# Five rooms instead of three for the transposed probabilities of heads 2 to 13

## The chip, the cores and the metric

The kernel runs on one core of a Trainium2 chip. The metric is device time in microseconds (us) of one execution; the median of several runs is compared. TensorE (PE) multiplies and transposes, VectorE (DVE) and ScalarE (ACT) work on what it leaves in PSUM, GpSimd (POOL) does elementwise work in SBUF, and SyncE (SP) issues nearly all DMAs.

## The reference

One transformer block on a sequence of 2048 rows of 1024 numbers, in float32: layer norm, attention with 16 heads of 64 and rotary embedding over a causal mask, output projection, layer norm and residual; then a gated feed-forward part with 2752 inner columns whose weights come as 4-bit codes with a scale for each 64, again with norms and residual.

```python
x = x + _layernorm(_L0_attn_ref(_layernorm(x, axis=-1), Wq, Wk, Wv, Wo), axis=-1)
x = x + _layernorm(_L0_ffn_ref(_layernorm(x, axis=-1), gate_codes, gate_scales, up_codes, ...), axis=-1)
...
logits = jnp.where(causal, logits, MASK_VAL) / jnp.sqrt(jnp.float32(HEAD_DIM))
attn = jax.nn.softmax(logits, axis=-1)
out = jnp.einsum('bhqk,bhkd->bhqd', attn, v)
```

## The kernel before

Matmuls take their operands as a rounded part and a remainder (fp32r, "hi" and "lo"); `split` makes the two: a cast on ACT (L118) and a subtraction on DVE (L119). A full product is three matmuls (`mm3`, L112 to L114).

The heads are worked off in pairs. For a head and a block of 512 queries (J), `scores` multiplies q by k (L273, L275) into one of three PSUM banks tagged "S", takes negated row maxima on DVE (L279, L281), exponentials on ACT (L283, `prob`), sums and reciprocals on DVE, and scales the probabilities on POOL (L305). `weighted` then goes over blocks of 128 keys (kb): four transposes (L315) put the probabilities of the block into one of three PSUM banks tagged "T" (`pt`); `split` casts and subtracts them into an SBUF room `pw` of 4 KB a partition, hi and lo; two matmuls (L319 with hi, L320 with lo) add the block to the output bank `o`. At the end ACT copies the lower half of `o` (L322) into `ol`, of which there is one room, DVE adds (L323) and SP stores it (L324). There are 640 such blocks, 480 of them in heads 2 to 13.

Between these instructions stand projections for later heads: `qkv` (L112 to L114 on `xc`, blocks of x loaded at L218, and on weights `w` cast by L184 from loads at L177).

SBUF is shared out as rooms by tag. `SLOTS` gives the number of rooms and KB of each: "pw" has 3 rooms of 4 KB, "pb" 2 of 4 KB. A new tile of a tag takes the room of the tile as many tiles back as the tag has rooms, and its first writer waits until that one's readers are done. "pb" holds weights of the second pair early on (until before head 2), and rows of the output projection (`y`, written at L467) from heads 14 and 15 on; between them it lies unused. 

The order of the instructions on each engine is not that of the source. A scheduler places them when the kernel is built, by its own account of durations and of free rooms and banks (`schedule_with_timeline_sim=True`), with priorities by place in the source and a few anchors that pace projections (`pace`, `after`). Each engine then runs its list in order. On the chip semaphores hold an instruction until its inputs and rooms are ready, and everything behind it on that engine waits as well.

Of the kernel before, what the change touches and what calls it, by code (L numbers as in the profile page):

```python
# [11 lines left out]
FR = mybir.dt.float32r  # L12
# [12 lines left out]
P = 128  # L25
KE = E // P
# [31 lines left out]
def block_kernel(ctx, tc, x, wq, wk, wv, wo, gu_codes, gu_scales, d_codes, d_scales, cos_sin, out):  # L58
# [15 lines left out]
    def slot(tag, shape, dtype, name):  # L74
        assert int(np.prod(shape[1:])) * 4 <= SLOTS[tag][1] * 1024, (tag, shape)
        return sb.tile(shape, dtype, tag=tag, name=name, bufs=SLOTS[tag][0])

    def bank(tag, name="bk"):
        return ps.tile([P, 512], F32, tag=tag, name=name, bufs=BANKS[tag])
# [37 lines left out]
    def split(hi, lo, src):  # L117
        A.copy(hi, src)  # L118
        return V.tensor_tensor(lo, src, f32(hi), ALU.subtract)  # L119
# [137 lines left out]
    def scores(J, q, k, anchors):  # L257
# [47 lines left out]
                    G.tensor_scalar(p, p, rc[:, jj % BATCH, i : i + 1], 0.0, ALU.mult, ALU.add)  # L305
        return prob

    def weighted(h, J, prob, v):
        o = bank("O", "o")
        nk = 4 * J + 4  # L310
        for kb in range(nk):
            j0 = max(0, kb - 4 * J)
            pt = bank("T", "pt")
            for j in range(j0, 4):
                T.transpose(pt[:, j * P : (j + 1) * P], prob[kb // 4][:, j, kb % 4 * P : (kb % 4 + 1) * P], ident)  # L315
            cs = slice(j0 * P, 512)
            pw = slot("pw", [P, 2, 512], FR, "pw")
            split(pw[:, 0, cs], pw[:, 1, cs], pt[:, cs])
            T.matmul(o[:, cs], lhsT=v[:, kb, :], rhs=pw[:, 0, cs], start=kb == 0, stop=False)  # L319
            T.matmul(o[:, cs], lhsT=v[:, kb, :], rhs=pw[:, 1, cs], start=False, stop=kb == nk - 1)  # L320
        ol = slot("ol", [D, 512], F32, "ol")
        A.copy(ol, o[D:P, :])  # L322
        V.tensor_tensor(ol, o[:D, :], ol, ALU.add)  # L323
        load(at[J][h * D : (h + 1) * D, :], ol)  # L324
# [45 lines left out]
    def attend(h, J, q, k, v, anchors):  # L370
        weighted(h, J, scores(J, q, k, anchors), v)
# [12 lines left out]
    for pair in range(KE - 1):  # L384
# [3 lines left out]
        for h in (2 * pair, 2 * pair + 1):  # L388
# [10 lines left out]
            for i, J in enumerate(order):  # L399
# [4 lines left out]
                if i % 2 == 0:  # L404
                    two = order[i : i + 2]
# [428 lines left out]
```

## Time and profile before

| what | value |
|---|---|
| median of 3 runs | 3020.89 us (3020.09 to 3022.32) |
| the profiled execution | 3012.18 us |
| its span | 3010.4 us |
| mean granted PE clock | 0.992 |
| PE, DVE, ACT, POOL busy | 97%, 68%, 56%, 32% of the span |
| all casts L118 of `pw` | 640, 324.1 us on ACT |
| all subtractions L119 of `pw` | 640, 378.4 us on DVE |
| all transposes L315 | 2176, 345.4 us on PE |

Busy time of an engine counts what its instructions cover. In a line of groups or waits, `A <- B: t, n, m` says that A sat idle until B ended, t us in total, n times, m us at the longest. A line of stretches gives the stretch, its length, busy us of PE, PEld (weight load), DVE, ACT and POOL with the number of instructions, then the granted PE clock, the busy share of the DMA engines and GB/s. A line of the chain gives start, length and what. Heads 2 to 13 fall into about 330 to 1345 us of the span.

### The profile page before, as it was taken

To read this page: it belongs to the slowest core of one execution; us is meant where nothing else is said; L and a number is where in the kernel's file an instruction comes from. 1 tells how busy PE (TensorE), PEld (TensorE's weight loads), DVE (VectorE), ACT (ScalarE), POOL (GpSimd) and SP (SyncE) were. 2 spreads that over 40 slices of the span, in tenths; PEclk is the share of its full clock that TensorE was granted. 3 is DMA by queue.
4 is the path that set the end of the run, shared out by engine and by line. 5 is a ranking of instruction groups with operands and counts; after the bars stand their busy time and mean duration, and the time that the engine had idled before them with its cause. 6 is when DMAs were issued, how large, how long until landed. Compare 5 with 4: busy or idle time off the path is not lost.

```text
span 3010.4 us, 42538 instructions
## 1 busy us (share of the span) xinstructions
PE 2912.1 (97%) x14168; PEld 2406.1 (80%) x14168; DVE 2032.5 (68%) x4171; ACT 1697.9 (56%) x3569; POOL 954.8 (32%) x1055
## 2 busy tenths in 40 slices
PE   7989999999998999999999999999999999999998
PEld 6868888787877787777787888888888888888886
DVE  6567778787867677777666667776666677444347
ACT  4256667776766666676565555655555566333234
POOL 5344344443444343454332121222221223100034
PEclk9999999999999999999999999999999999999999
DMA  8787665657557558472356344434434444744446
GB/s 295 271 255 233 213 214 186 213 171 226 157 196 195 172 176 254 139 229 90 123 178 230 109 138 139 154 129 140 135 121 135 139 151 151 255 140 144 150 144 234
DMA packets 271740, 536.01 MB, mean 178 GB/s; under 512 B 22944, under 2 KB 113056, under 8 KB 255648
## 3 DMA queue, kind: packets, MB, share of 16 engines
q1 hardware_dynamic: 269344, 529.10, 54.3%
q10 hardware_dynamic: 2176, 4.19, 0.4%
q8 instruction: 112, 1.84, 0.3%
q14 instruction: 108, 0.88, 0.1%
HBM read 371.98 MB, written 161.22 MB: 177 GB/s over the span
## 4 chain that ended last, share of the span: by engine, by line
PE 79%; DMA 9%; DVE 5%; ACT 2%; issue 1%; POOL 1%; SPq 1%; POOLq 0%; ACTq 0%; DVEq 0%
PE bk L112 14%; PE bk L114 14%; PE bk L113 14%; PE pt L315 6%; PE qkv L112 4%; PE qkv L114 4%; PE qkv L113 4%; PE o L320 3%; PE o L319 3%; PE s L273 3%; PE s L275 3%; PE pj L466 2%; PE pj L464 2%; PE pj L465 2%; DMA wf<-in_wq 2%
## 5 line engine op out<-in xcount | busy, mean ns | idle before, releaser
L305 POOL TENSOR_SCALAR prob<-prob,rc 128x512 f32<-128x512 f32 (+3 forms) x640 | 404.9, 659 | 440.1 <-DVE rc L300 231.0
L112 PE MATMUL bk<-x,wt 128*128 128x512 f32 x1376 | 534.1, 390 | 4.6 <-ACT x L118 3.7
L113 PE MATMUL bk<-x,wt 128*128 128x512 f32 x1376 | 535.9, 389 | 0.0
L114 PE MATMUL bk<-x,wt 128*128 128x512 f32 x1376 | 535.7, 389 | 0.0
L283 ACT ACTIVATE prob<-s,mxs 128x512 f32<-128x512 f32 (+3 forms) x640 | 402.6, 633 | 145.9 <-DVE mxs L281 88.7
L119 DVE TENSOR_TENSOR pw<-pt,pw 128x512 fp32r<-128x512 f32 (+3 forms) x640 | 378.4, 601 | 119.7 <-ACT pw L118 117.9
L529 ACT ACTIVATE ln<-cs,bias 128x512 f32<-128x512 f32 x520 | 359.8, 716 | 107.0 <-DVE mb L535 20.4
L118 ACT CAST pw<-pt 128x512 fp32r<-128x512 f32 (+3 forms) x640 | 324.1, 527 | 169.6 <-PE pt L315 137.0
L315 PE MATMUL pt<-ident,prob 128*128 128x128 f32 x2176 | 345.4, 275 | 7.3 <-DVE pw L119 6.0
L315 PEld LDWEIGHTS pt<-ident,prob 128*128 128x128 f32 x2176 | 267.6, 141 | 62.0 <-issue 7.7
L112 PEld LDWEIGHTS bk<-x,wt 128*128 128x128 f32 x1376 | 258.4, 188 | 59.1 <-ACT x L118 3.9
L114 PEld LDWEIGHTS bk<-x,wt 128*128 128x128 f32 x1376 | 258.7, 188 | 53.9
L113 PEld LDWEIGHTS bk<-x,wt 128*128 128x128 f32 x1376 | 258.8, 188 | 53.5
L281 DVE TENSOR_REDUCE mxs<-s 128x1 f32<-128x512 f32 x384 | 260.9, 681 | 58.6 <-PE s L275 57.3
L273 PE MATMUL s<-k,q 128*128 128x512 f32 (+3 forms) x640 | 265.0, 415 | 23.9 <-ACT prob L283 19.7
L320 PE MATMUL o<-pw,v 128*128 128x512 f32 (+3 forms) x640 | 247.0, 388 | 8.3 <-DVE pw L119 7.6
L319 PE MATMUL o<-pw,v 128*128 128x512 f32 (+3 forms) x640 | 243.8, 381 | 8.6 <-ACT pw L118 6.7
L112 PE MATMUL qkv<-xc,w 128*128 128x512 f32 x576 | 230.9, 401 | 11.8 <-ACT w L184 6.3
L113 PE MATMUL bk<-bt,at 128*128 128x512 f32 x616 | 239.6, 389 | 0.0
L114 PE MATMUL bk<-bt,at 128*128 128x512 f32 x616 | 238.8, 389 | 0.0
L112 PE MATMUL bk<-bt,at 128*128 128x512 f32 x616 | 238.6, 389 | 0.0
L275 PE MATMUL s<-k,q 128*128 128x512 f32 (+3 forms) x640 | 235.6, 371 | 0.0
(150 smaller groups left out, 5504.7 us busy)
## 6 DMA issues: line engine op xcount, KB each, us to landing
xc<-xd SPq DMA_DIRECT2D x96, 1024.0 KB, 9.1
q<-qs SPq DMA_DIRECT2D x128, 256.0 KB, 6.8
ast<-S SPq DMA_DIRECT2D x44, 512.0 KB, 3.7
cs<-in_gu_scales SPq DMA_DIRECT2D x172, 128.0 KB, 3.2
cs<-in_gu_codes SPq DMA_DIRECT2D x86, 256.0 KB, 3.0
A<-in SPq DMA_DIRECT2D x66, 256.0 KB, 2.1
S<-in SPq DMA_DIRECT2D x66, 256.0 KB, 3.1
ast<-A SPq DMA_DIRECT2D x33, 512.0 KB, 4.5
```

What stands on the lines that cost most here:

```text
L112: r = T.matmul(o, lhsT=w[:, 0], rhs=xx[:, 0], start=first, stop=False)
L113: T.matmul(o, lhsT=w[:, 0], rhs=xx[:, 1], start=False, stop=False)
L114: T.matmul(o, lhsT=w[:, 1], rhs=xx[:, 0], start=False, stop=last)
L119: return V.tensor_tensor(lo, src, f32(hi), ALU.subtract)
L273: mm = T.matmul(s, lhsT=q[:, 0, j * P : (j + 1) * P], rhs=k[:, b:e], start=True, stop=False)
L275: T.matmul(s, lhsT=q[:, 1, j * P : (j + 1) * P], rhs=k[:, b:e], start=False, stop=True)
L283: A.activation(prob[i][:, j, : e - b], s, AF.Exp, bias=mx, scale=sign, accum_out=sums[:, j % BATCH, i : i + 1])
L305: G.tensor_scalar(p, p, rc[:, jj % BATCH, i : i + 1], 0.0, ALU.mult, ALU.add)
L315: T.transpose(pt[:, j * P : (j + 1) * P], prob[kb // 4][:, j, kb % 4 * P : (kb % 4 + 1) * P], ident)
L319: T.matmul(o[:, cs], lhsT=v[:, kb, :], rhs=pw[:, 0, cs], start=kb == 0, stop=False)
L320: T.matmul(o[:, cs], lhsT=v[:, kb, :], rhs=pw[:, 1, cs], start=False, stop=kb == nk - 1)
L529: A.activation(ln, c8, AF.Prelu, bias=bias_of[ab], scale=ab[0], alpha=ab[2])
```

## The change

`weighted` counts its blocks in `parts_made`. In heads 2 to 13 (`KE` is 8) two of every five blocks take their room from "pb" instead of "pw". With three rooms of "pw" and two of "pb", a block there takes the room of the block five back instead of three back. The numbers of rooms, the instructions and their sizes stay as they are.

```diff
+    parts_made = [0]
+
     def weighted(h, J, prob, v):
         o = bank("O", "o")
         nk = 4 * J + 4
@@
             cs = slice(j0 * P, 512)
-            pw = slot("pw", [P, 2, 512], FR, "pw")
+
+            parts_made[0] += 1
+            two = 2 <= h < 2 * KE - 2 and parts_made[0] % 5 > 2
+            pw = slot("pb" if two else "pw", [P, 2, 512], FR, "pw")
             split(pw[:, 0, cs], pw[:, 1, cs], pt[:, cs])
```

## The prediction

> **What bounds the kernel now.** I read the page first, then its engines by stretch, then the waits inside the stretch that the change touches (330 to 1345 us, heads 2 to 13), then the chain there.
>
> ```profile
> span 3010.4 us, 42538 instructions
> PE 2912.1 (97%) x14168; PEld 2406.1 (80%) x14168; DVE 2032.5 (68%) x4171; ACT 1697.9 (56%) x3569; POOL 954.8 (32%) x1055
> ```
>
> The stretch (its length, then busy us of PE, PEld, DVE, ACT, POOL, the granted clock, DMA share, GB/s):
>
> ```profile
> 330.00:1345.00 1015.00, 973.61 (x5301) 806.88 (x5300) 770.99 (x1995) 688.43 (x1824) 430.43 (x590) 0.99 0.63 195
> ```
>
> TensorE (PE) is the bound. In the stretch it idles 1015.0 - 973.6 = 41.4 us. Nothing in this change alters how much PE has to do, so only that idle time, and the clock lost after it, can be won.
>
> Who waits, in the stretch, for PE and then for ScalarE (ACT):
>
> ```profile
> PE s L273 <- ACT prob L283: 15.1, 23, 2.1
> PE qkv L112 <- ACT w L184: 5.4, 3, 3.9
> PE o L319 <- ACT pw L118: 5.1, 4, 2.6
> PE qkv L112 <- DMA xc<-xd: 4.8, 4, 1.8
> PE o L320 <- DVE pw L119: 4.6, 14, 0.7
> ```
>
> ```profile
> ACT pw L118 <- PE pt L315: 98.9, 134, 5.0
> ...
> ACT pw L118 <- PE o L320: 23.3, 15, 3.7
> ...
> ACT ol L322 <- DMA at<-ol: 11.5, 6, 2.4
> ```
>
> The wait for a free room is the line "ACT pw L118 <- PE o L320": the cast waits until the second weighted matmul of the block three back has read its room, 15 times, 23.3 us. No line of PE's is that wait; PE waits for the exponentials (L283), for weights (L184) and x blocks from DMA, and for casts and subtractions.
>
> What PE does in the three longest room waits (ACT resumes at 524.2, 662.5 and 820.0 us):
>
> ```profile
> 520.00:525.00 5.00, 5.00 (x31) 4.40 (x30) 0.71 (x6) 1.30 (x4) 4.13 (x7) 1.00 0.85 290
> 658.00:663.00 5.00, 5.00 (x26) 4.04 (x25) 1.45 (x3) 1.88 (x6) 0.00 (x0) 1.00 0.39 131
> 816.00:821.00 5.00, 5.00 (x26) 4.08 (x25) 1.31 (x3) 1.67 (x5) 0.00 (x0) 1.00 0.41 133
> ```
>
> PE (second number) is busy in all of the 5 us: it runs projection matmuls, and the hold on ACT costs nothing there. Last, the longest pieces of the chain that ended last in this stretch:
>
> ```profile
> 527.01 9.37 DMA at<-ol
> ...
> 729.71 13.64 DMA wf<-in_wq
> ...
> 931.23 12.17 DMA wf<-in_wq
> ...
> 1250.01 8.86 DMA at<-ol
> ```
>
> They are loads of weights, and the store of a head's output, whose single room `ol` holds up the next head's copy on ACT.
>
> **The change part by part.** *Removed: the room wait.* With five rooms I laid the built orders of both kernels side by side. In the old order 45 of the 480 casts of heads 2 to 13 have their transposes placed ahead of the matmul that frees their room; in the new one none has. So the wait does go away: between 0 (what the three stretches show) and 23.3 us (if every hold were on the path, and a little more with the clock). Following each PE wait of over 0.06 us back from releaser to releaser, I find one that passes through such a hold, at 430.9 us, 0.39 us. I take **-0.4 us**. The rooms are free: the weights in `pb` are last read long before head 2 (PE's 142nd us of work against the 328th), and the first row block that reuses `pb` is written at 1378.4 us, after head 13.
>
> *Moved: the order.* The scheduler places instructions by its own account of time, so freeing rooms reorders 4,308 of the 14,168 PE instructions, 126 of SP's and 74 of POOL's by a few places, up to the 1515th us of PE's work, past heads 14 and 15 too. PE's work is the same (2,832 us at 227 ns a 512-column matmul, 110 ns a transpose, by the starts in the trace). I count, for each weighted matmul, how much PE work lies between the end of its block's transposes and itself (its lead), and give each class of lead the mean stall that class had in the trace (time between starts above those figures):
>
> ```
> lead us            <0.5   0.5-1  1-1.5  1.5-2  2-2.5  2.5-3  3-4
> first (L319) old   3      10     36     74     77     36     103
>  stall us in all   2.3    0.6    3.8    3.9    1.6    0.9    2.2
>  new               1      5      34     66     83     51     95
> second (L320) old  3      0      11     18     65     72     92
>  stall us in all   1.5    0      2.5    0.1    5.4    2.1    1.5
>  new               1      2      7      18     49     75     103
> ```
>
> At the old means the first lose 2.1 us and the second 2.9: **-5.0 us**. The same for score matmuls against the one three back in their PSUM bank: 31 old leads under 2 us with 16.8 us of stalls become 33, 28 of 2 to 2.5 us become 37, 67 of 2.5 to 3 become 53: **+0.4 us**. These means hold only as far as the causes do: most of the score stalls are ACT held by something else. Bounds of this part: -30.2 (all stalls of weighted matmuls, longer leads included, gone) and +5 (the classes' means are no better than their mirror).
>
> *The store of a head's output.* ACT's copy L322 waits for the landing of the store before. In the trace that comes 11 to 12 us after the end of the earlier output's last matmul (679.0 to 690.1, 836.5 to 847.4, 524.2 to 536.4, 1248.1 to 1258.9), and the copy is late where two outputs end closer. In the new order short pairs come closer still: 5.99 to 5.19 us of PE work, 5.76 to 5.19 twice, 4.98 to 3.39, 6.81 to 5.56, and three new ones near 6 (from 9 to 12). Queued behind the copy on ACT are casts and exponentials, and PE waits for these. But what counts is PE work from the earlier end to the first matmul that needs ACT past the copy: 9.2 to 8.3 us (the pair at 530 us), 12.2 to 12.7 twice, 11.9 to 12.1, 11.9 to 9.0 (1255 us), 12.9 to 11.3 (617 us, where SP also issues three loads ahead of the store), and the pair at 1193 us opens up and loses its 1.2 us of stalls. By pair, with a release at 11 to 12 us, 0.6 for the copy and 0.6 to 0.9 for the next piece: 0, -1, -0.2, +2, +1.5, -1.2. **+1 us**, between -3 and +7.
>
> *SP's queue.* At 931 to 939 us the second weight load (`wf` of Wk) moves ahead of two loads of k; the chain 931.2 to 953.6 us carries 4.4 us of PE stalls (2.8 and 1.6). Two issues of 0.6 us earlier: **-1.5 us**, from 0 to -4.4. Loads of x blocks: their leads grow by 0.2 to 2.3 us at four stalled places and shrink by 2.5 at one (1018.9 us): **+0.5 us**, -2.7 to +2.5. At 1656 us, after heads and projection, two casts come ahead of three others that wait for codes: **-1 us** of a 3.9 us stall (0 to -3.9).
>
> Sum: -0.4 - 5.0 + 0.4 + 1.0 - 1.5 + 0.5 - 1.0 = **-6.0 us**. The profiled execution took 3012.18 us, its span 3010.4 and 1.8 around it, so it would take 3006.2. The median of the three timed runs is 8.7 us above the profiled one; with the difference carried over, 3020.9 - 6.0 = **3014.9 us**. A 0.2% change, about what a measurement of this kernel tells from none, is 6.0 us: the sum sits on that edge.
>
> A rule speaks for far more. The Trainium skill, Perfetto Trace Analysis, Identifying Performance Opportunities, says that the same gap repeating on the engine that should be saturated can mean too few buffers for the next tile. By that rule the 41.4 us of idle would be the rooms' and the time would be 2979.5 us; the row of PE's waits does not name the rooms, and the stretches at 520, 658 and 816 us show them full and PE busy.
>
> **The rivals.** *The holds are on the path after all.* A held cast holds the exponentials behind it, and the 15.1 us of PE waits for those might shrink with the holds. For it: 23.3 us of holds, and PE's clock falls to 0.77 in 530 to 545 us just after one. Against: no chain passes through them. Price: 23.3 us, less the share hidden (a quarter) = -18: 3003 us.
>
> *The output store decides: slower.* One mechanism: with more blocks under way, the end of one output moves closer to the next while `ol` still has one room; ACT waits at L322 and everything behind it. Place: the short pairs at 530, 617, 686, 843, 1008 and 1255 us. It decides as soon as the store lands later than about 11 us after the earlier output's end, as at 530 us, where PE lost 2.35 us (537.8). Six pairs at that 2.35 us more are +14, less the 4 that the other terms then still give: +10, 3031 us.
>
> *It does not do what it says.* Three PSUM banks still take the transposes, so a block cannot run further ahead than the subtraction (L119) that frees a bank; in the new order the transposes still follow the matmul three back by the same 0.45 us of PE work (median). Then the rooms stay unused but for a few casts: 0, 3021 us.
>
> **How the numbers follow.** Forecast 48% (half of it on each side of -6 us, a twentieth above +6), holds 16%, store 24%, nothing 12%. Faster by over 0.2%: 24 + 16 = 40%. Slower: 24 + 2 = 26%. Within: 22 + 12 = 34%. The forecast's own range is 3007 to 3023 us; reaching to both outer rivals, 3003 to 3031 leaves about two in ten out.
>
> **What would show it.** Right: "ACT pw ... <- PE o" falls from 23.3 us to under 5 in this stretch while PE's busy time stays at 2912 and its idle falls by only some 5 us; PE's waits for pw (5.1 + 4.6) fall by about half; "ACT ol <- DMA at<-ol" stays near 11.5. Wrong: PE's wait for prob (15.1) falls by most of itself (first rival), or "ACT ol <- DMA at<-ol" doubles with PE's wait for prob above 20 (second).

## The result and the profile after

The change made the kernel a little slower: 3027.72 us (median of 12 runs, 3021.34 to 3038.45) against 3021.61 of the kernel before on the same chip (12 runs), ratio 1.0028, 95% interval 1.0017 to 1.0040. By the ratio that is +8.4 us (the two medians lie 6.1 us apart) where -6 was forecast. One profiled execution lies up to some 10 us from its kernel's median, so sizes below rest on ratios, and traces are compared stretch by stretch.

The page, then the stretch 330 to 1345 us (columns as before):

```profile
span 3019.4 us, 42495 instructions
PE 2915.4 (97%) x14168; PEld 2408.5 (80%) x14168; DVE 2037.4 (67%) x4171; ACT 1696.1 (56%) x3569; POOL 957.5 (32%) x1055
```

```profile
330.00:1345.00 1015.00, 971.64 (x5289) 805.20 (x5289) 774.65 (x1993) 684.81 (x1822) 431.57 (x589) 0.99 0.62 193
```

PE idles 43.4 us there instead of 41.4. Who waits, for PE and then for ACT (L315 and what follows it in `weighted` has moved down by 2 to 5 lines: L317 transposes, L324 and L325 weighted matmuls, L327 copy, L329 store):

```profile
PE s L273 <- ACT prob L283: 14.5, 25, 3.5
PE qkv L112 <- DMA xc<-xd: 5.7, 4, 2.2
PE o L325 <- DVE pw L119: 5.3, 11, 1.0
PE qkv L112 <- ACT w L184: 5.0, 4, 2.2
PE o L324 <- ACT pw L118: 3.6, 3, 2.8
```

```profile
ACT ol L327 <- DMA at<-ol: 23.5, 10, 4.9
...
ACT pw L118 <- PE o L325: 3.8, 3, 2.8
```

The room wait has all but gone, as forecast (23.3 to 3.8 us). PE's waits for `pw` are not halved (9.7 to 8.9 us), and ACT's wait for the store of a head's output has doubled (11.5 to 23.5). The largest of these, at the 617 us pair, as the timeline shows it (start, length, instruction, in brackets the idle time before it and what ended it):

```profile
616.12 0.55 SPq L329 DMA_DIRECT2D at<-ol  x1
...
625.29 0.58 ACT L327 COPY ol<-o 64x512 f32<-64x512 f32 x1 [4.93 <-DMA at<-ol]
...
626.73 0.45 PE L273 MATMUL s<-k,q 128*128 128x384 f32 x1 [3.46 <-ACT prob L283]
```

The store issued at 616.12 us lands 9.09 us later, the next head's copy stands 4.93 us, the exponentials behind the copy are late, and PE stands 3.46 us for them.

### The profile page after: what moved, and what is told of

It reads as the page before. It is cut to its first block, busy times and chain, and to the rows that moved or that the text cites. A ratio compares the mean times of both kernels' runs of the same rounds, so it can differ in the third digit from the quotient of the medians.

```text
span 3019.4 us, 42495 instructions
## 1 busy us (share of the span) xinstructions
PE 2915.4 (97%) x14168; PEld 2408.5 (80%) x14168; DVE 2037.4 (67%) x4171; ACT 1696.1 (56%) x3569; POOL 957.5 (32%) x1055
## 4 chain that ended last, share of the span: by engine, by line
PE 75%; DMA 11%; DVE 7%; ACT 3%; issue 2%; POOL 2%; SPq 1%; POOLq 0%; ACTq 0%; DVEq 0%
PE bk L113 14%; PE bk L114 14%; PE bk L112 14%; PE pt L317 6%; PE qkv L112 4%; PE qkv L114 4%; PE qkv L113 4%; PE o L325 3%; PE o L324 3%; PE s L273 3%; PE s L275 3%; DMA wf<-in_wq 2%; DMA at<-ol 1%; DMA xc<-xd 1%; DVE st L129 1%
## 5 line engine op out<-in xcount | busy, mean ns | idle before, releaser
L317 PE MATMUL pt<-ident,prob 128*128 128x128 f32 x2176 | 344.6, 274 | 10.8 <-DVE pw L119 10.3
L317 PEld LDWEIGHTS pt<-ident,prob 128*128 128x128 f32 x2176 | 266.2, 141 | 65.9 <-issue 9.1
L325 PE MATMUL o<-pw,v 128*128 128x512 f32 (+3 forms) x640 | 246.1, 386 | 10.9 <-DVE pw L119 10.2
L324 PE MATMUL o<-pw,v 128*128 128x512 f32 (+3 forms) x640 | 242.8, 380 | 5.3 <-ACT pw L118 4.0
```

## The experiments

Each kernel was timed beside the kernel before on one chip; ratios are to it, with their 95% intervals. Kernels with pinned queues add the lines below to five rooms: each instruction of an engine is tied behind the one that is to stand in front of it. The tie is for the scheduler alone and adds no semaphore. `PINS` holds the wanted order, taken from the built kernels before and after.

```diff
+    no_wait = mybir.DependencyInfo(mybir.DependencyClass.NoSync, mybir.DependencyReason.DATA)
+    for engine in PINS:
+        ids = [f"I-{n}" for n in pinned(engine) if f"I-{n}" in made]
+        for one, two in zip(ids, ids[1:]):
+            tc.add_manual_dep(made[two], one, no_wait, reason="order")
```

**The store, and the extent.** *store_first*: in the kernel after, the x-block load (L218) in front of the 617 us store is tied behind that store; 64 PE places move with it.

```diff
+            if len(loads) == 41:
+                after(ins, stores[19])
```

> The changed kernel with one order forced: in SP's queue the 1 MB load of an x block in the projection of the third pair is placed behind the store of head 4's last output instead of ahead of it (64 of 14,168 PE instructions move with it, 5 of SP's). Theory A (the single room of the output store holds ACT): the store lands some 3 us earlier after its issue, ACT's wait at the next copy (4.9 us, at 625 us) falls to under 2, PE's stall at 626.7 us (3.7 us, and the half-clock stretch after it) falls to under 1, and the run is 4 to 6 us faster than the changed kernel, 3022 us where that takes 3027. Theory B (the new order loses a little in many places, and no site decides): within 2 us of the changed kernel.

1.0027 (1.0016 to 1.0038). In its trace ACT's wait at the copy fell from 4.93 to 1.51 us, PE's behind it from 3.46 to 1.37, and the 484 to 633 us stretch from 155.3 to 151.4 us, but the total did not follow: the ratio is that of the change. Inside the pinned orders the same move did count (new_617_store_ahead, below); why it did not here stays open. A second room for the output goes further. *two_out_rooms*:

```diff
+            if not outs:
+                outs.append(slot("ol", [P, 512], F32, "ol"))
+            outs.append(0)
+            mine, other = (slice(0, D), slice(D, P)) if len(outs) % 2 else (slice(D, P), slice(0, D))
+            ol = outs[0][mine, :]
+            A.copy(ol, o[other, :])
```

> The changed kernel with two rooms for the output of a head in heads 2 to 13 (partitions 0 to 63 and 64 to 127 of one tile, used in turn, the sum built from the other half first). Theory A: ACT's waits for the store (23.5 us in 330 to 1345 us) fall under 3 us, PE's wait for prob (14.5 us) by a third or more, and the run is 6 to 12 us faster than the changed kernel, at or below the kernel before: 3016 to 3021 us. Theory B: the waits for the store vanish and others take their place; within 4 us of the changed kernel, 3023 to 3031 us.

1.0059 (1.0045 to 1.0073): slower still, though ACT's wait for the store fell to 0.8 us. PE's waits in the stretch:

```profile
PE qkv L112 <- DMA xc<-xd: 11.6, 5, 3.2
PE qkv L112 <- ACT w L184: 11.5, 4, 4.5
```

Both have doubled: where the wait for the store went, waits for x blocks and weights stand. The scheduler made yet another order for this kernel (over 2000 PE places differ from the kernel after), so the run does not tell the second room from that order. *rooms_heads_2_5* and *rooms_heads_6_13* give the five rooms to a part of the heads:

```diff
-            two = 2 <= h < 2 * KE - 2 and parts_made[0] % 5 > 2
+            two = 2 <= h < 6 and parts_made[0] % 5 > 2
```

> Five rooms in heads 2 to 5 alone. Up to head 5 the order is that of the changed kernel, with the store behind the three loads at 616 us. Theory A: this alone gives the 6 to 7 us that the changed kernel has lost by 630 us, and nothing comes back after it: 3026 to 3029 us. Theory B: the loss is spread, so a third of the heads with five rooms lose a third: 3023 to 3024 us.

> Five rooms in heads 6 to 13 alone; up to head 5 the order of the kernel before. Theory A: without the site at 616 us the rest of the change is worth what the two traces show after 630 us: 3 us gained up to head 13, and 2 to 6 us lost behind it: 3018 to 3025 us. Theory B: two thirds of the loss, 3025 to 3026 us.

1.0014 (1.0003 to 1.0024) and 1.0017 (1.0006 to 1.0028): each carries about half of the loss; it is not at one place.

**Rooms or order?** *five_rooms_old_order*: five rooms, all five queues pinned to the places of before.

> The kernel after, with the five rooms left as they are, but every instruction of all five engines' queues pinned to the place that it had in the kernel before (42 thousand instructions, no place differs from before). It takes the scheduler's new order away and keeps the rooms. Theory C (the new order, spread over the heads, is what costs): the time is that of before, ratio 1.000 within 0.001; the room wait "ACT pw <- PE o" falls from 23.3 us to under 10, "ACT ol <- DMA at<-ol" stays near before's 11.5, and at the same place in TensorE's work the lead of the run is within 3 us of before's everywhere. Rival C2 (five rooms cost by themselves, whatever the order): the ratio stays at 1.003, some 3026 us when before is at 3018. Were the room wait on the path after all, it would be 0.996 or less.

1.0005 (0.9997 to 1.0014): no measurable change. ACT's waits:

```profile
ACT ol L535 <- DMA at<-ol: 12.0, 6, 2.8
ACT pw L326 <- PE o L533: 7.6, 5, 3.7
```

The room wait falls by 15.7 us and the time not at all: the holds were hidden, and the rooms themselves cost nothing that these runs can tell. The loss belongs to the order. Then the two mixed orders, and a reshuffle of the kernel before:

```diff
-PACE = 0.85
+PACE = 0.84
```

> Five rooms; the queues of TensorE, ScalarE, VectorE and GpSimd pinned to the places of before, the SP queue (loads and stores) pinned to the places of after, which differ in 126 of 1426. It puts in the new order of the DMAs alone. If the place of the loads and stores in the SP queue is what costs (the store at 617 us behind three loads, the store at 1255 us): ratio 1.002 to 1.004, and "ACT ol <- DMA at<-ol" near after's 23.5 us. If the order of the computing is: 0.999 to 1.001, and that wait nearer to before's 11.5 us.

> Five rooms; the queues of TensorE, ScalarE, VectorE and GpSimd pinned to the places of after, the SP queue to those of before: the other half of the order. If the DMA order costs: ratio 0.999 to 1.001. If the order of the computing costs: 1.002 to 1.004. If a mismatch of the two costs, both mixed kernels are slower than after, 1.004 or more.

> The kernel before with three rooms and PACE at 0.84 for 0.85: no room and no wait is added or removed, but the scheduler's order moves in 2790 TensorE places (the change moved 4245). It measures what a reshuffle does by itself. Theory D (the chip's time scatters by some 0.2% with any reshuffle, and the five rooms' order is one such draw): the ratio differs from 1 by 0.001 to 0.004, either way. Theory C (the order planned with more rooms is tighter than the chip's loads allow): 1.000 within 0.001, since three rooms plan no tighter than before.

1.0074 (1.0061 to 1.0087) and 1.0085 (1.0073 to 1.0097): the mixtures are worse than either order, so SP's list and the computing have to fit, and these two runs do not say which half costs. The reshuffle gives 1.0005 (0.9994 to 1.0016): moving 2790 PE places need not cost anything.

**Which stretch?** The two orders have places up to which both have issued exactly the same instructions on all engines. Between such places I put the new order into the old one, stretch by stretch.

> Five rooms, all five queues pinned to the order of before, except from the start of head 2's stretch to TensorE work position 434 (about 484 us), where they have the order of after (478 TensorE, 102 ScalarE, 181 VectorE, 13 SP places). It asks in which stretch the order costs. Theory C (the loss sits at a few sites where the new order puts a load or store later than the work that needs it, the first at 617 us): this stretch has none in the traces, so the ratio is that of the five rooms in the old order, 1.0005 within 0.001. Rival E (a little everywhere, in proportion to the moved instructions): 11% of the 0.0023 that the order costs, 1.0008.

> As above with the new order from work position 434 to 571 (about 484 to 633 us; 703 TensorE and 33 SP places), the stretch in which the store of a head's output stands behind three loads in the SP queue and lands at 625 us. Theory C: this stretch holds most of the loss, +6 us, ratio 1.002 to 1.0025, with the stall of TensorE at 617 to 627 us as in after. Rival E: 17% of the loss, 1.0009.

> As above with the new order from work position 571 to 1099 (about 633 to 1224 us; 1982 TensorE and 47 SP places, nearly half of what the change moves). In the profiled runs after gains about 9 us on before here, but five rooms in the old order already differ by 6 us from before in the same stretch with the same order, so part of that is chance. Theory C: this stretch gains 3 to 8 us, ratio 0.998 to 0.9995 and faster than both kernels. Rival E: it holds 47% of the loss, 1.0016.

> As above with the new order from work position 1099 (about 1224 us) to the end (1082 TensorE and 33 SP places): the pair of stores at 1255 us, heads 14 and 15, and the stretch at 1650 us. Theory C: +5 to +8 us, ratio 1.002 to 1.003, as after's run against before's in this stretch. Rival E: 25% of the loss, 1.0011.

In this order: 1.0008 (0.9996 to 1.0020), 1.0024 (1.0015 to 1.0033), 0.9980 (0.9971 to 0.9990), 1.0035 (1.0022 to 1.0048). Less the 1.0005 of five rooms in the old order these are +0.0003, +0.0019, -0.0025 and +0.0030, each within about 0.001; together +0.0027, where the change, less the same 0.0005, has +0.0023. The loss is two stretches, and between them the new order wins. Then the two stretches were cut finer:

> new_order_617 with three places of the SP queue changed and nothing else: the store of the head's output at 613.9 us goes ahead of the load of xc and the load of q that stood in front of it. If the place of the store is what costs in this stretch (theory C): the stretch from position 434 to 571 falls from 154.4 us to 150 to 151.5 us, and the ratio from 1.0024 to 1.0005 to 1.0012. If the order of the computing or the other 30 moved loads cost: it stays at 1.002 or above.

> Five rooms, all queues pinned to the order of before except from work position 1099 to 1142 (about 1224 to 1272 us), which has after's order: 77 TensorE and 2 SP places. It cuts the last stretch, which cost 0.0030, in two. Theory C: the pair of stores at 1255 us, where the copy waits for the store that came before it and TensorE for the cast behind the copy, costs 3 us (this stretch took 46.9 to 48.3 us in five runs of the old order and 50.6 to 51.2 us in the new): ratio 1.0015 within 0.001. Rival E (in proportion to what moved): 7% of that loss, 1.0007.

> The other part of the last stretch: after's order from work position 1142 (about 1272 us) to the end (1005 TensorE and 31 SP places), before's elsewhere. Theory C: the load of the output weights for heads 14 and 15 is waited for 2 us longer at 1350 us, and the queries at 1313 us by 1 us: this stretch up to position 1231 took 105.2 to 108.6 us in the old order and 109.2 to 110.0 us in the new, +3.5 us and some 2 us behind it, ratio 1.002 within 0.001. Rival E: 93% of the last stretch's loss, 1.0033.

1.0000 (0.9990 to 1.0009), 1.0014 (1.0005 to 1.0022), 1.0022 (1.0012 to 1.0033). Three places in SP's list are the whole loss at 617 us; the pair at 1255 us and heads 14 and 15 share that of the end. Rival E, a little everywhere, is out: of the 4245 PE places that the change moves (the forecast counted 4,308) the middle has 1982, 47%, and gains. The 77 places at 1255 us, 2%, carry +0.0009; as a ratio that is not clear of the noise, but the traces below have that stretch 2.8 us longer without overlap.

**A version that wins?** *rooms_heads_6_11* leaves the scheduler free and gives five rooms to those heads alone; the other two are pinned.

```diff
-            two = 2 <= h < 2 * KE - 2 and parts_made[0] % 5 > 2
+            two = 6 <= h <= 11 and parts_made[0] % 5 > 2
```

> Five rooms for heads 6 to 11 alone (before has three in all, the change five in heads 2 to 13), no pinned queue: the scheduler's own order then equals before's up to TensorE work position 642 and from 1142 to 1231, and after's between 830 and 1016, where the new order took 3 to 5 us less in the traces. Theory C (the sites decide): the gain of the middle without the losses at 617 us, 1255 us and 1350 us, ratio 0.998 within 0.001, faster than before and than after. Rival E (a little everywhere): heads 6 to 11 carry six of the twelve heads' loss, 1.0014.

> The two harmless pieces together: five rooms, all queues pinned to the order of before, except from work position 434 to 1099 (about 484 to 1224 us), which has after's order with the store of 613.9 us ahead of the two loads in front of it. If the stretches add up: five rooms in the old order 1.0005, less 0.0025 for the middle, less 0.0005 for the stretch of 617 us with its store ahead, 0.9975 within 0.001, faster than before. Rival: the middle's gain was a draw of that one kernel (five rooms in heads 6 to 11 kept the 5 us in its stretch and was 0.9998 in all): 0.9995 to 1.0005.

> new_order_middle once more, unchanged, beside the other on one chip. If its gain is the order's: 0.998 within 0.001 again. If it was a draw of the runs it was compared with: 0.9995 to 1.0005.

0.9998 (0.9989 to 1.0007), 0.9976 (0.9962 to 0.9990), 0.9988 (0.9976 to 1.0000). The first missed: its order differs from both in places, and it is no better than before. The second is where the sum of its stretches put it (0.9975), by the ratios some 7 us below before and 16 below after. The middle repeated gave 0.9988 after 0.9980: a gain again, by less, with an interval that ends at 1. On that chip the medians of these two are 5.8 and 6.0 us below before, so the 617 us stretch with its store ahead added nothing that can be told.

## Why the prediction was wrong

Places are given by PE work: the time that the matmuls issued up to there take together, so that one place has one number in all kernels. The stretches in the traces (us between the first matmul's start at either end, executions with one and the same PE order put together, the two mixtures left out):

| PE work, us | about, us of the span | old order: mean, range (executions) | new order |
|---|---|---|---|
| 434 to 571 | 485 to 634 | 149.7, 148.1 to 151.7 (11) | 154.9, 154.4 to 155.3 (3); store ahead 149.7, 150.6 |
| 571 to 1099 | 634 to 1225 | 592.2, 587.9 to 597.0 (8) | 586.0, 581.2 to 589.8 (4) |
| of it 830 to 1016 | 917 to 1129 | 212.2, 210.4 to 213.8 (9) | 207.7, 206.0 to 210.9 (7) |
| 1099 to 1142 | 1225 to 1272 | 47.6, 46.9 to 48.3 (9) | 50.4, 49.0 to 51.2 (4) |
| 1142 to 1231 | 1272 to 1378 | 106.1, 105.1 to 108.6 (11) | 110.8, 109.2 to 112.2 (5) |

Together +6.5 us (+5.2 - 6.2 + 2.8 + 4.7), beside +8.4 by the ratio, or +6.9 for the order alone (0.0023). The steps in turn:

- *Room wait, -0.4: right.* Five rooms in the old order are worth nothing that can be measured. The Trainium skill, Perfetto Trace Analysis, Identifying Performance Opportunities, says that a gap repeating on the engine to be saturated can mean too few buffers. Taken for all of PE's idle time, that gave 2979.5 us; five_rooms_old_order, with the buffers, is at 3019.04. The gaps that repeated for want of a room were ACT's (7.6 of 23.3 us are left), and the time shows no wait of PE, the engine to be saturated, for them.
- *Leads, -5.0: the step that failed first.* PE's waits for `pw` were to fall by half from 9.7 us. They are 8.9 in after and 8.0 in new_order_middle, but five_rooms_old_order, where no lead has changed, has 8.8 as well:

```profile
PE o L533 <- DVE pw L327: 4.9, 15, 0.7
PE o L532 <- ACT pw L326: 3.9, 3, 2.8
```

  So the longer leads won nothing that shows. A class's mean stall was not what an instruction gained by changing class. That the stalls sit in a few matmuls with a late load or store behind them, so that lead in the others wins nothing, fits the chains but was not tested by itself.
- *Output store, +1.0: mechanism right, the term mis-sized.* It was +1.5 at 617 us and +2 at 1255; the stretches measured +5.2 and +2.8. This is the second rival's mechanism, at two of its six pairs. Its total is near for another reason (+10, measured +8.4): no loss shows at its other four pairs (with the store at 617 us ahead, the stretch that also holds the 530 us pair is as long as in the old order, and the middle with the other three is shorter), and PE's wait for prob did not rise above 20 us (14.5).

  At 1255 us it went as the forecast had it, and the store itself lands no later. PE's order is what differs, in before and then in after:

```profile
1258.95 0.58 ACT L322 COPY ol<-o 64x512 f32<-64x512 f32 x1 [2.17 <-DMA at<-ol]
1261.85 0.50 PE L273 MATMUL s<-k,q 128*128 128x512 f32 x1 [0.64 <-ACT prob L283]
```

```profile
1256.66 0.58 ACT L327 COPY ol<-o 64x512 f32<-64x512 f32 x1 [2.13 <-DMA at<-ol]
1258.18 0.50 PE L324 MATMUL o<-pw,v 128*128 128x512 f32 x1 [2.82 <-ACT pw L118]
```

  ACT's copy waits as long in both. In before PE runs twelve projection matmuls meanwhile and then waits 0.64 us; in after the weighted matmul, whose cast stands behind the copy, comes ahead of the projections, and PE waits 2.82 us. From 1258.88 us the granted clock is 0.5 for 3.41 us; in before it stays at 1.00 from 1250 to 1270 us.

Two things were missed at 617 us. First, where the release comes from. I took 11 to 12 us after the earlier output; in these traces the store lands when all that SP issued before it has landed. The issue and landing of the same DMAs in both pinned kernels, from their traces:

```
                          issued   landed
new_order_617   q         612.05   618.31
                xc        612.80   621.46
                q         613.28   622.14
                store     613.89   622.32
store_ahead     q         612.87   619.09
                store     614.69   619.27
                xc        615.26   622.40
                q         615.85   623.37
```

In both the store lands 0.18 us behind what was issued before it; with the x block and a q load out of its way that is 4.58 us after its issue instead of 8.43. The copies it holds up, in new_order_617 and in new_617_store_ahead:

```profile
622.40 0.58 ACT L526 COPY ol<-o 64x512 f32<-64x512 f32 x1 [4.29 <-DMA at<-ol]
```

```profile
619.38 0.58 ACT L526 COPY ol<-o 64x512 f32<-64x512 f32 x1 [0.46 <-PE o L524]
```

The forecast did note the three loads ahead of the store and gave them no price. Second, the clock. The stretches 620 to 624, 624 to 628 and 628 to 632 us, of new_order_617 and then of new_617_store_ahead (length, PE busy and matmuls first, the clock in the third column from the right):

```profile
620.00:624.00 4.00, 1.18 (x9) 0.81 (x6) 1.34 (x5) 1.57 (x5) 2.23 (x4) 0.87 1.03 349
624.00:628.00 4.00, 4.00 (x12) 2.77 (x13) 3.88 (x11) 4.00 (x14) 0.00 (x0) 0.50 1.05 355
628.00:632.00 4.00, 4.00 (x19) 3.23 (x19) 2.91 (x9) 2.38 (x7) 0.00 (x0) 0.77 1.05 266
```

```profile
620.00:624.00 4.00, 3.33 (x21) 2.34 (x19) 3.92 (x12) 3.19 (x9) 3.01 (x5) 1.00 1.03 324
624.00:628.00 4.00, 4.00 (x24) 3.38 (x25) 4.00 (x13) 3.99 (x13) 0.00 (x0) 1.00 1.04 363
628.00:632.00 4.00, 4.00 (x27) 3.34 (x26) 4.00 (x13) 3.17 (x9) 2.16 (x4) 1.00 1.05 307
```

After a wait of 2.82 us PE is "busy" for all of the next 4 us with 12 matmuls instead of 24. By these rows the half clock costs an estimated 4 x (1 - 0.50) + 4 x (1 - 0.77) = 2.9 us more than the idle time itself; the sum had only idle time in it. The Trainium skill, TensorE: Matmul & The Clock Gate, Part 1: The HAM clock gate, puts the fall behind at least one idle window of about 3.4 us; here a wait of 2.82 us, in a span in which PE was busy for 1.18 of 4 us, was enough, and the clock falls at 622.99 us, before that wait is over (623.84 us).

- *x blocks, +0.5: wrong in sign, and where most of the gain lies.* The forecast let the lead shrink at 1018.9 us. In five_rooms_old_order the copy behind a store and then an x block come late there, and the clock falls; in new_order_middle the same x block (the 72nd of 96) is issued at 1008.75 instead of 1015.85 us, of which 2 us are that execution being ahead (830 us of PE work at 922 instead of 924 us). The two PE waits of the old order (in new_order_middle neither is left, though ACT's copy still waits 2.19 us for the store, after 2.75), then the 12 us around them in the old and in the new order:

```profile
1022.68 0.50 PE L481 MATMUL s<-k,q 128*128 128x512 f32 x1 [1.27 <-ACT prob L491]
1025.74 0.79 PE L320 MATMUL qkv<-xc,w 128*128 128x512 f32 x1 [1.66 <-DMA xc<-xd]
```

```profile
1018.00:1030.00 12.00, 9.07 (x34) 6.59 (x33) 6.83 (x17) 4.74 (x12) 6.21 (x11) 0.79 0.81 248
```

```profile
1016.00:1028.00 12.00, 11.90 (x61) 9.67 (x61) 9.59 (x29) 7.40 (x19) 8.07 (x13) 1.00 0.82 247
```

  Of the middle's 6.2 us, 4.5 lie between 830 and 1016 us of PE work. Cut finer, the place itself, 905 to 918 us of PE work, took 18.8 us (16.9 to 20.4) in the eight executions with the old order and 15.1 (14.6 to 15.5) in the four with the new one, 3.7 us less. No kernel with the new order at this site alone was run.
- *SP's weight load, -1.5, and 1656 us, -1.0:* not seen. PE's wait for weights is 5.0 us after 5.4, and what follows work position 1231 took 1620.6 and 1622.5 us in before and five_rooms_old_order and 1624.8 in after.
- *Heads 14 and 15: no term at all.* The forecast said that the order moves there and gave it no price; it is +4.7 us in the traces, at two places where a load is waited for longer. PE at 1300 to 1320 us in five_rooms_old_order and in new_order_heads_14_15:

```profile
PE qkv L320 <- DMA xc<-xd: 0.3, 1, 0.3
```

```profile
PE s L471 <- DMA q<-qs: 3.2, 1, 3.2
```

  And ACT's second cast of the output weights, behind which casts of `pw` are queued, in the same two:

```profile
1350.54 1.04 ACT L637 CAST wo<-wof 128x1024 fp32r<-128x1024 f32 x1 [3.65 <-DMA wof<-in_wo]
```

```profile
1356.72 1.04 ACT L627 CAST wo<-wof 128x1024 fp32r<-128x1024 f32 x1 [4.73 <-DMA wof<-in_wo]
```

  In after the wait for q is 1.3 us. At the first place (1163 to 1171 us of PE work) all eleven executions with the old order took 8.2 us, the five with the new one 9.9 to 11.8: +2.4 us on the mean. PE waits for that q load in none of the eleven and in four of the five; in the fifth, store_first, it waits 1.8 us for exponentials. The wait for the output weights is 2.0 to 4.5 us in the old order and 3.8 to 5.0 in the new, so the two overlap there; 1205 to 1215 us of PE work takes 1.6 us more on the mean. No run set either place right by itself, so at heads 14 and 15 the cause is read from the traces and not shown.

So -6.0 had the sign of one stretch, for another cause than it gave, and lacked what decides at the others: the queue in front of a store or load, and the clock after the wait.

## What to carry to other kernels

Freeing a buffer in a kernel that a scheduler orders is two changes: the buffer, and a new order everywhere behind it. Pinning the old order with the new buffer separates them in one run, and where the wait was hidden the order is all that is left. Price a new order first by its DMA queue: look for every store or load that something on the busiest engine's chain waits for, and add up what is issued in front of it. Then look at how much of that engine's work still covers the landing, as at 1255 us.

## What the hardware showed unexpectedly

- Of the 402 DMAs that SP issued between 330 and 1345 us before (397 after), none landed before one issued earlier. In the table at 617 us a 256 KB load of q landed 0.7 to 1.0 us after what stood in front of it and a 1 MB x block 3.1 us, and the store of 128 KB waited for both.
- Identical queues do not run identically. The stretch 571 to 1099 of PE work took between 587.9 and 597.0 us in eight executions with the old order; a gain of 5 us cannot be read from one trace of each kernel.
